# Both rope products of a key in one GpSimd instruction, behind two ScalarE copies

## The chip, the cores and the metric

The kernel runs on one core of a Trainium2 chip. A core has a matrix engine (TensorE, PE in the profile; its weight loads are PEld), a vector engine (VectorE, DVE), an activation engine (ScalarE, ACT), a general engine (GpSimd, POOL) and an engine that only issues transfers (SyncE, SP). Each works through its own queue in order; they meet at semaphores. The metric is the device time of one execution in microseconds, as the median of several runs.

## What is computed

One transformer block over 2048 tokens of width 256, in float32: attention with a compressed key-value path and rotary positions, a residual and a layer norm; then a mixture of 16 experts, of which each token takes two, with a shared expert, a residual and a second layer norm. Cut to what the change touches:

```python
q = (x @ Wq) ...                      # 16 heads of 16, 4 without rotation, 12 with
c_kv = x @ Wkv_down                   # 64 wide
k = (c_kv @ Wk_up) ...
v = (c_kv @ Wv_up) ...
q_rope, k_rope = _apply_rope(q_rope, cos, sin), _apply_rope(k_rope, cos, sin)
scores = jnp.einsum('bhqd,bhkd->bhqk', qf, kf) * scale    # causal
out = jnp.einsum('bhqk,bhkd->bhqd', softmax(scores), v)
```

A rotated key is the sum of two products: the plain projection times a table of cosines, and a projection with its even and odd columns exchanged times a table of signed sines.

## The kernel before

Tokens are taken in four chunks of 512 (`CH`), heads in four groups of four (`G`). The channels of a head are padded to 32 rows (`PAD`), so a group of four heads fills 128 partitions. Everything about keys and queries lies with channels on partitions and tokens along the free dimension, as 128x512 tiles.

For each group `g` and chunk `c`, `project_k` (L422) makes a key tile. PE writes two PSUM banks `pk[0]` and `pk[1]` (the plain and the exchanged projection; 64 rows of weights each). DVE reads `pk[0]`, adds the column `unit` (a one in one row of each head, which carries the softmax shift later) and multiplies by the cosines `cs[c][:, 0]` (L430). For the very first key DVE also does the second product (L434). For the other 15, ACT copies `pk[1]` to SBUF (L436), since POOL doesn't read PSUM, and POOL multiplies that copy by the sines in place (L437). Then POOL adds the halves into the key (L439). The two halves are the two planes of one tile `tmp`, named `rot` in the profile, of which there is one buffer.

Queries are made likewise (`project_q`: copy on ACT, L452, product on POOL, L453), values by `project_v` (ACT, L468).

The attention itself is a list of steps, written out by hand (`steps`, L605 to L669). A step may hold a `Maxima` part and a `Weighted` part. `Maxima` computes scores of four heads with the queries as rows (`m`), only to find the row maxima: DVE reduces each bank (L505), or, on the diagonal, masks and reduces it (L500). `Weighted` computes scores with the keys as rows (`s`); ACT takes the exponential (L550), and on the diagonal POOL masks it (L554). The product with the values (`av`) of a step is put on PE after the scores of the step that follows; ACT copies it out (`more`, L581, two buffers) and POOL adds it to a sum (L582), or DVE adds it from PSUM where a step has no maxima (L578).

The maxima are turned by PE and added to the queries (`shift`, L515 to L523, `qa`). Projections are hung behind steps by number (`put`, L683 to L719): the keys of group `g` come 14, 11, 8 and 6 steps ahead of the first maxima step of that group's last chunk.

All PSUM of this stage is one pool of eight banks taken in turn (`bank`, L404; tag `sc`). So a matmul that takes a bank waits until what took that bank eight takings earlier has been read. In a full step the takings are `s` and `m` of heads in turns (two `s`, two `m`, two `s`, two `m`), then `av`, then whatever is hung behind the step. Matmuls keep their written order (L142); the other engines' queues are ordered when the program is built, by what is ready. Each float32 product is two passes on PE.

At the start, weights and rope tables come over SP's queue (L350 to L382), and POOL copies parts of the weights of groups 1 to 3 as they land (`double`, L339, hung behind step 5).

Of the kernel before, what the change touches and what calls it, by code (L numbers as in the profile page):

```python
# [12 lines left out]
AF = mybir.ActivationFunctionType  # L13
ALU = mybir.AluOpType
# [36 lines left out]
def block_kernel(  # L51
# [14 lines left out]
    nc = tc.nc  # L66
# [25 lines left out]
    cs = [const.tile([P, 2, CH], F32, tag=f"cs{c}", name=f"cs{c}") for c in range(3)]  # L92
# [52 lines left out]
    def matmul(*args, **kw):  # L145
        pe(nc.tensor.matmul, *args, **kw)
# [142 lines left out]
    with ExitStack() as att:  # L289
# [14 lines left out]
        unit = ap1.tile([P, 1], F32, tag="unit", name="unit")  # L304
# [99 lines left out]
        def bank(name):  # L404
            return ps_sc.tile([P, CH], F32, tag="sc", name=name)
# [16 lines left out]
        def project_k(g, c):  # L422
            tmp = wk1.tile([P, 2, CH], F32, tag="rot", name=f"rot{g}_{c}")
            pk = [bank(f"pk{g}_{c}_{a}") for a in range(2)]
            for a in range(2):
                r = slice(a * LAT, (a + 1) * LAT)
                matmul(
                    pk[a], lhsT=wks[g][r], rhs=ckv[c][r], start=True, stop=True
                )
            nc.vector.scalar_tensor_tensor(  # L430
                tmp[:, 0, :], pk[0], unit, cs[c][:, 0, :], ALU.add, ALU.mult
            )
            if (g, c) == (0, 0):
                nc.vector.tensor_tensor(tmp[:, 1, :], pk[1], cs[c][:, 1, :], ALU.mult)  # L434
            else:
                nc.scalar.copy(tmp[:, 1, :], pk[1])  # L436
                nc.gpsimd.tensor_tensor(tmp[:, 1, :], tmp[:, 1, :], cs[c][:, 1, :], ALU.mult)  # L437
            ks[g, c] = kv.tile([P, CH], F32, tag="k", name=f"k{g}_{c}")
            nc.gpsimd.tensor_tensor(ks[g, c], tmp[:, 0, :], tmp[:, 1, :], ALU.add)  # L439

# [245 lines left out]
        for step, what, c in (  # L686
            (1, project_k, 1), (1, project_q, 1), (3, prologue, 2), (4, project_v, 0),
            (6, project_k, 2), (7, prologue, 3), (9, project_v, 1), (9, project_q, 2),
            (14, project_k, 3), (17, project_q, 3), (19, project_v, 2), (32, project_v, 3),
        ):  # L690
            if what is prologue:
                put(step, what, c)
            else:
                put(step, what, 0, c)
# [498 lines left out]
```

## Time and profile before

| what | value |
|---|---|
| three runs | 780.91, 782.22, 784.98 us; median 782.22 |
| the profiled execution | 787.57 us, span 785.7 us |
| mean granted TensorE clock | 0.979 |
| ACT, exponentials (L550), 640 | 292.2 us busy |
| DVE, maxima off the diagonal (L505), 384 | 238.2 us busy, 0.683 each |
| POOL, sums of value products (L582), 125 | 136.8 us busy; 1.270 at 512 columns, 0.727 at 256 |
| DVE, first product of a key (L430), 16 | 12.0 us busy |
| ACT, copy of the second half (L436), 15 | 8.8 us busy |
| POOL, second product (L437), 15 | 19.1 us busy |
| POOL, sum of the halves (L439), 16 | 20.3 us busy |

A line of the timeline gives the start, the duration, the engine, the line of the kernel, the operation with its output and input, how many of it are merged, and in brackets how long the engine had been idle and which instruction ended that. A line of the table by stage gives the stretch, its length, then the busy time and number of instructions of PE, PEld, DVE, ACT and POOL, the granted clock, the DMA share and the GB/s. In a tile's view the three durations are the least, the median and the largest in ns, and "who waited for it" gives microseconds and times. Matmuls overlap and their ends are modelled, so PE's busy share overstates how hard it works.

### The profile page before, as it was taken

What the parts mean: (1) busy time and instruction counts of PE and PEld (TensorE: products, weight loads), DVE (VectorE), ACT (ScalarE), POOL (GpSimd) and SP (SyncE); (2) the same over time, 40 slices, a digit from 0 to 9 for tenths busy, and PEclk for the clock granted to TensorE, in tenths of its full rate; (3) what the DMA queues carried; (4) which work ended last, traced back from release to release, by engine and by line L of the source; (5) the groups of instructions that cost most, each with busy time, mean ns of one, the idle gap of its engine ahead of it and who ended that gap; (6) DMA issues with size and microseconds to landing.
All of it is one profiled execution on the core that took longest, in us unless ns stands there. A gap on an engine that the chain in (4) does not pass through costs nothing.

```text
span 785.7 us, 14672 instructions
## 1 busy us (share of the span) xinstructions
PE 754.0 (96%) x5074; PEld 366.7 (47%) x5074; DVE 525.0 (67%) x1435; ACT 453.6 (58%) x987; POOL 359.9 (46%) x589
## 2 busy tenths in 40 slices
PE   7999999999999999999999999999998989999994
PEld 3444443444434334443434454444333658887542
DVE  2658798887687787767787768788657633333275
ACT  1244747377786787777788767875553202223356
POOL 3234536535377454657645564553446124445300
PEclk9999999989999999999999999998989999999998
DMA  5469999998000000001000000000115543332172
GB/s 148 131 149 263 300 291 291 293 308 214 2 1 1 1 1 3 1 4 36 20 1 1 2 1 2 2 1 2 55 55 144 112 123 102 112 105 64 29 225 98
DMA packets 75981, 72.54 MB, mean 92 GB/s; under 512 B 20890, under 2 KB 70141, under 8 KB 75904
## 3 DMA queue, kind: packets, MB, share of 16 engines
q1 hardware_dynamic: 70936, 62.43, 29.9%
q0 software_dynamic: 3504, 8.43, 3.2%
q10 hardware_dynamic: 1464, 0.72, 0.4%
q8 instruction: 41, 0.67, 0.4%
q14 instruction: 36, 0.29, 0.1%
HBM read 27.09 MB, written 45.65 MB: 93 GB/s over the span
## 4 chain that ended last, share of the span: by engine, by line
PE 81%; SPq 5%; DVE 4%; DMA 3%; issue 3%; ACT 2%; POOL 1%; ACTq 0%; POOLq 0%; DVEq 0%
PE s L143 23%; PE av L143 18%; PE m L143 16%; PE py L143 4%; PE ab L143 4%; PE pq L143 3%; PE c L143 2%; PE pk L143 2%; PE ph L143 2%; SPq L326 1%; PE pv L143 1%; SPq L325 1%; PE pz L143 1%; PE px L143 1%; PE h L143 1%
## 5 line engine op out<-in xcount | busy, mean ns | idle before, releaser
L550 ACT ACTIVATE p<-s 128x512 f32<-128x512 f32 (+3 forms) x640 | 292.2, 540 | 93.9 <-PE m L143 48.8
L143 PE MATMUL m<-k,q 32*128 32x512 f32 (+3 forms) x1280 | 298.0, 570 | 0.7 <-DVE rot L430 0.5
L143 PE MATMUL s<-qa,k 32*128 32x512 f32 (+3 forms) x1280 | 282.9, 569 | 3.5 <-DVE avs L578 2.5
L505 DVE TENSOR_REDUCE pm<-m 128x1 f32<-128x512 f32 x384 | 238.2, 683 | 61.1 <-PE m L143 59.9
L582 POOL TENSOR_TENSOR avs<-avs,more 128x512 f32<-128x512 f32 (+3 forms) x125 | 136.8, 1094 | 140.2 <-ACT more L581 136.5
L143 PEld LDWEIGHTS s<-qa,k 32*128 32x128 f32 x1280 | 108.8, 187 | 120.9 <-ACT p L550 69.1
L143 PE MATMUL av<-p,v 128*32 128x512 f32 (+3 forms) x1280 | 158.7, 551 | 1.6 <-POOL p L554 0.6
L500 DVE CUSTOM_DVE_ANT_0 m<-m,qmask 128x512 f32<-128x512 f32 (+3 forms) x256 | 118.5, 522 | 37.2 <-PE m L143 34.0
L143 PEld LDWEIGHTS m<-k,q 32*128 32x128 f32 x1280 | 120.2, 184 | 38.3 <-issue 12.0
L554 POOL TENSOR_SCALAR_AFFINE_SELECT p<-p 128x128 f32<-128x128 f32 x256 | 70.3, 296 | 36.8 <-ACT p L550 35.1
L581 ACT COPY more<-av 128x512 f32<-128x512 f32 (+3 forms) x125 | 65.8, 526 | 34.8 <-PE av L143 27.9
L143 PEld LDWEIGHTS av<-p,v 128*32 128x32 f32 x1280 | 27.9, 108 | 107.3 <-ACT p L550 53.6
L954 POOL DMA_INDIRECT yg<-yb,to x41 | 40.4, 986 | 71.5 <-ACT yb L942 50.6
L281 POOL DMA_INDIRECT xg<-xr,slot x32 | 31.1, 973 | 33.2 <-issue 21.2
L143 PE MATMUL h<-xT,cs 128*128 128x512 f32 (+1 forms) x96 | 43.3, 597 | 2.4 <-ACT u L808 1.4
L143 PE MATMUL py<-w2r,hT 112*128 112x256 f32 (+1 forms) x164 | 39.8, 380 | 0.0
L500 DVE DVE_READ_ACCUMULATOR2_ANT pm<- 128x1 f32 x256 | 36.2, 142 | 0.0
L143 PEld LDWEIGHTS py<-w2r,hT 112*128 112x128 f32 x164 | 30.8, 190 | 6.1 <-ACT hT L993 0.5
L143 PE MATMUL ab<-xT,w 128*112 128x256 f32 x128 | 32.9, 380 | 0.0
L143 PE MATMUL pq<-xT,wqs 128*128 128x512 f32 x64 | 31.7, 618 | 0.0
L143 PEld LDWEIGHTS h<-xT,cs 128*128 128x128 f32 (+1 forms) x96 | 16.9, 180 | 24.2 <-issue 18.8
L437 POOL TENSOR_TENSOR rot<-rot,cs 128x512 f32<-128x512 f32 x15 | 19.1, 1273 | 17.1 <-DMA cq<-in_rope_dram 7.4
(166 smaller groups left out, 651.8 us busy)
## 6 DMA issues: line engine op xcount, KB each, us to landing
xg<-hot SPq DMA_DIRECT2D x16, 2064.0 KB
xb<-xg SPq DMA_DIRECT2D x16, 258.0 KB
got<-yg SPq DMA_DIRECT2D x8, 512.0 KB
w<-in_w_dram SPq DMA_DIRECT2D x4, 896.0 KB
xr<-in_x_dram SPq DMA_DIRECT2D x4, 512.0 KB
w<-in_w_dram SPq DMA_DIRECT2D x4, 512.0 KB
out_dram<-o SPq DMA_DIRECT2D x8, 256.0 KB
w2r<-in_w_dram SPq DMA_DIRECT2D x1, 1792.0 KB
```

The costliest lines, as they stand in the source:

```text
L143: tc.keep_in_program_order(op(*args, **kw))
L281: put = nc.gpsimd.indirect_dma_start(out=xg[:, :], out_offset=bass.IndirectOffsetOnAxis(ap=slot[:, j, i : i + 1], axis=0), in_=xr[c][:, t, ...
L325: queue.dma_start(out=cs[c][r : r + LOW], in_=of[:LOW])
L326: queue.dma_start(out=cs[c][r + LOW : r + PAD], in_=of[NOPE:HD])
L437: nc.gpsimd.tensor_tensor(tmp[:, 1, :], tmp[:, 1, :], cs[c][:, 1, :], ALU.mult)
L500: nc.vector.tensor_tensor_reduce(out=ps[:, :n], in0=ps[:, :n], in1=qmask[:, CH - n :], scale=1.0, scalar=3.0 * NEG, op0=ALU.add, op1=ALU.m ...
L505: nc.vector.tensor_reduce(to, ps, AX.X, ALU.max)
L550: nc.scalar.activation(pr[:, n0:], ps[:, n0:], AF.Exp, scale=SCALE)
L554: nc.gpsimd.affine_select(out=diag, in_=diag, pattern=[[1, P]], base=0, channel_multiplier=-1, compare_op=ALU.is_ge, fill=0.0,)
L581: nc.scalar.copy(more[:, n0:], pv[:, n0:])
L582: nc.gpsimd.tensor_tensor(to, to, more[:, n0:], ALU.add)
L954: nc.gpsimd.indirect_dma_start(out=yg[:, :], out_offset=bass.IndirectOffsetOnAxis(ap=to, axis=0), in_=yb, in_offset=None, bounds_check=2 * ...
```

## The change

For 15 of the 16 keys the addition of `unit` and the first product leave DVE. ACT now makes two copies, the first an Identity with `unit` as its bias, and POOL multiplies both planes of `tmp` by both planes of the rope table in one instruction of 1024 columns. The first key stays as it was. The sum of the halves isn't touched.

```diff
-            nc.vector.scalar_tensor_tensor(
-                tmp[:, 0, :], pk[0], unit, cs[c][:, 0, :], ALU.add, ALU.mult
-            )
             if (g, c) == (0, 0):
+                nc.vector.scalar_tensor_tensor(
+                    tmp[:, 0, :], pk[0], unit, cs[c][:, 0, :], ALU.add, ALU.mult
+                )
                 nc.vector.tensor_tensor(tmp[:, 1, :], pk[1], cs[c][:, 1, :], ALU.mult)
             else:
+                nc.scalar.activation(tmp[:, 0, :], pk[0], AF.Identity, bias=unit)
                 nc.scalar.copy(tmp[:, 1, :], pk[1])
-                nc.gpsimd.tensor_tensor(tmp[:, 1, :], tmp[:, 1, :], cs[c][:, 1, :], ALU.mult)
+                nc.gpsimd.tensor_tensor(tmp, tmp, cs[c], ALU.mult)
             ks[g, c] = kv.tile([P, CH], F32, tag="k", name=f"k{g}_{c}")
             nc.gpsimd.tensor_tensor(ks[g, c], tmp[:, 0, :], tmp[:, 1, :], ALU.add)
```

## The prediction

> **What bounds the kernel now.** I read the page's busy shares, then its chain of waits, then the busy time by stage, then the tile view of the two projections of a key, and last the timeline around each of the 15 changed keys.
>
> ```profile
> PE 754.0 (96%) x5074; PEld 366.7 (47%) x5074; DVE 525.0 (67%) x1435; ACT 453.6 (58%) x987; POOL 359.9 (46%) x589
> PE 81%; SPq 5%; DVE 4%; DMA 3%; issue 3%; ACT 2%; POOL 1%; ACTq 0%; POOLq 0%; DVEq 0%
> 216.00:250.00 34.00, 33.75 (x280) 13.20 (x276) 26.39 (x64) 26.51 (x59) 24.82 (x33) 1.00 0.00 1
> ```
>
> PE holds 81% of the chain, DVE 4%. In the stretch 216 to 250 us, which contains four changed keys, PE is busy 33.75 of 34 us, DVE 26.4, ACT 26.5, POOL 24.8. So the work taken from DVE is mostly work nobody waits for; what counts is what PE waits for. The tile view of `pk` says that:
>
> ```profile
> L430 DVE SCALAR_TENSOR_TENSOR rot<-pk,unit,cs x16: 741/751/752, 14.2 to 378.2; 128x512 f32<-128x512 f32 x16
> L436 ACT COPY rot<-pk x15: 586/586/587, 23.7 to 378.2; 128x512 f32<-128x512 f32 x15
> ...
>   PEld m L143: 3.9, 14
> ```
>
> The last line stands under "who waited for it": PE waits 3.9 us in 14 places for `pk` to be read. The reason is the ring of eight PSUM banks: the two banks of `pk` are the last two taken in their step, so eight takings later they come up as the last two `m` products of the next step. What PE waits for is the reading of `pk`, not the key: in every pass but the first the finished key is wanted several steps later.
>
> **The terms taken away and added, per key.** DVE loses one 0.75 us instruction (15 x 0.75 = 11.2 us). ACT gains one Identity. The trace has no Identity of 128x512 with one column operand. From below, the copy of this shape takes 0.586 and the exponential 0.602. From above, the Identity of 128x256 with two column operands (L1042) takes 0.591 against 0.384 for the Silu of 112x256 without any (L927): 0.207 for two, so 0.10 for one, and 0.81 if one cost as much as both. I take 0.60 + 0.10 = 0.70, bounds 0.59 to 0.81. POOL's multiplication goes from 512 to 1024 columns: by L582 at 256 and 512 columns (0.727 and 1.270) a column costs 2.12 ns, so 1.27 + 512 x 2.12 = 2.36 us, 1.09 more; from above two instructions, 2.54; from below 2.3, as the three widths of L582 lie on one line. ACT's four exponentials of 0.602 take 2.07 together, so each starts 0.11 before its forerunner ends.
>
> **Before 52 us: nothing.** Two changed keys lie here (reads at 23.7 and 39.5 us). The stretch ends with POOL copying weights that arrive late behind the issues of the SP queue, and with PE's `av` behind that:
>
> ```profile
> 51.25 0.39 POOL L348 COPY wqs<-sines 128x48 f32<-128x48 f32 x2 [1.60 <-DMA sines<-in_wq_dram]
> 51.59 0.55 POOL L554 TENSOR_SCALAR_AFFINE_SELECT p<-p 128x128 f32<-128x128 f32 x2
> 51.94 1.98 PE L143 MATMUL av<-p,v 128*32 128x512 f32 x5 [0.44 <-POOL p L554]
> ```
>
> The chain runs through SP's issues from 17.4 to 48.3 us, and the change issues no DMA and adds none behind which one waits. POOL idles 3.3 us before 47.2, so the 1.7 us by which a key gets later (Identity's 0.70 less the overlap of 0.11, and POOL's 1.09) is covered; without that cover it would cost up to 1.7 each.
>
> **Two keys where DVE is the limit: a gain.** At 70.5 and 105.8 us the steps are without exponentials before, and DVE works without a gap:
>
> ```profile
> 68.13 2.48 DVE L505 TENSOR_REDUCE pm<-m 128x1 f32<-128x512 f32 x4
> 70.53 0.74 DVE L430 SCALAR_TENSOR_TENSOR rot<-pk,unit,cs 128x512 f32<-128x512 f32 x1
> 71.18 2.58 DVE L505 TENSOR_REDUCE pm<-m 128x1 f32<-128x512 f32 x4
> ```
>
> The last four `m` start at 71.32, right behind L430. ACT is free from 68.23 and would have read both banks by 69.4, so those matmuls can follow the last `s` (70.66 plus the 0.1 to 0.2 that separates starts). That is 0.5 us each; bounds 0 (the exponentials on ACT start 69.42 anyway) and 0.65, DVE's start to start. Two: -1.0.
>
> **Nine keys in full steps: a loss.** From 116 to 371 us the read of `pk` stands in a gap of both engines. Around 230 us:
>
> ```profile
> 230.10 0.59 ACT L436 COPY rot<-pk 128x512 f32<-128x512 f32 x1 [0.42 <-PE pk L143]
> 230.13 0.75 DVE L430 SCALAR_TENSOR_TENSOR rot<-pk,unit,cs 128x512 f32<-128x512 f32 x1 [0.66 <-PE pk L143]
> 230.93 0.18 PEld L143 LDWEIGHTS m<-k,q 32*128 32x128 f32 x1 [0.23 <-DVE rot L430]
> 231.11 2.07 ACT L550 ACTIVATE p<-s 128x512 f32<-128x512 f32 x4 [0.43 <-PE m L143]
> 231.99 0.16 PEld L143 LDWEIGHTS av<-p,v 128*32 128x32 f32 x8 [0.76 <-issue]
> ```
>
> Now the banks are read side by side, free at 230.69 and 230.88. After the change ACT reads them in turn: Identity 230.10 to 230.80, copy from 230.69 to 231.28. The first `m` loses nothing, the second starts at 231.33, not 230.94. Behind it in PE's queue is `av`, which needs all rows and so waits for it. The second pass of that `m` moves from 231.46 to at least 231.33 + 0.43 = 231.76. PE is late by 0.30 to 0.39; I take 0.35. ACT's exponentials start at 231.17, not 231.11: nothing. DVE gains nothing, as its next reduction waits 0.32 for PE already. Lateness of a PE that is busy all the time isn't made up. Bounds per key: 0.2 (Identity at 0.59, passes closing up) and 0.5 (Identity at 0.81). Nine: +3.15.
>
> **Two keys ahead of a diagonal step of 128 columns: a loss on POOL.** At 246 and 378 us POOL's queue holds the mask of the next values product:
>
> ```profile
> 247.34 1.28 POOL L437 TENSOR_TENSOR rot<-rot,cs 128x512 f32<-128x512 f32 x1
> 248.56 0.30 POOL L554 TENSOR_SCALAR_AFFINE_SELECT p<-p 128x128 f32<-128x128 f32 x1
> 248.83 1.27 POOL L439 TENSOR_TENSOR k<-rot 128x512 f32<-128x512 f32 x1
> 250.04 0.80 POOL L554 TENSOR_SCALAR_AFFINE_SELECT p<-p 128x128 f32<-128x128 f32 x3
> ```
>
> PE's `av` on these masks runs from 250.65 to 251.24, so there is no slack. After: copies end 247.55, product 247.60 to 249.96, one mask to 250.23, the add to 251.5, the other masks to 252.3, `av` done near 252.6. That is 1.35 late (the PE lateness of the paragraph above lies inside it). If the order of POOL's queue changes so that all four masks precede the add, they end at 251.05 and 0.35 remains; upper bound 1.75, with the product at 2.54 and Identity at 0.81. Two: +2.7. Elsewhere the masks have room: at 137 us they would end near 139.5, with their `av` at 140.15.
>
> **Sum.** -1.0 + 3.15 + 2.7 = +4.85 us. The profiled execution took 787.57 us (span 785.7), which is 5.35 above the median of 782.22; I add the sum to the median: 787.1. By the bounds: +0.7 x 2 - 1.3 + 1.8 - 0.7 = +1.2 to 0 + 4.5 + 3.5 = +8.0, so 783.4 to 790.2.
>
> **A rule weighed.** Identity between exponentials could bring table loads. In the trace the Identity at 761.98 follows a Silu and that at 774.67 a Sqrt, neither with a load, so I count none. A load, where there is one, takes 1.28 us, and the Silu at 761.49 starts 0.02 after it. The Trainium skill, "ScalarE: Activation LUTs", What ACT_TABLE_LOAD costs, adds a drain of 1.38 us to each switch, 2.66 in all; the trace shows no such drain. A pair of loads at each of 13 keys would cost 13 x 2 x 1.28 = 33 us by the row. By that page it would be 69.
>
> **The rivals.**
> 1. Faster, 0.17. PE's waits on L430 vanish and nothing takes their place, because ACT has the second copy done before PE comes to that `m`. For it: ACT idles 0.4 on both sides of the copy in most places. Against: the two reads together last 1.18 us, and PE arrives 0.84 after the first begins. It decides at 0.84 for both reads. Price: the 3.9 us of `pk` waits and 1.0 of the DVE stretch go: 777.3.
> 2. Lost in the noise, 0.13. PE's lateness is taken up by the small gaps ahead of later `av`, and POOL puts the masks first: -1.0 + 9 x 0.1 + 2 x 0.35 = +0.6: 782.8.
> 3. POOL becomes the bound, 0.08. Its queue delays every `avs` sum, the two `more` buffers fill, ACT waits. POOL's load in 216 to 250 rises by 4 x 1.09 to 29.2 of 34 us, which speaks against it. 13 keys x 1.7 = +22: 804.3.
> 4. Identity brings a pair of table loads at each key, 0.02: 13 x 2 x 1.28 = +33: 815.6.
>
> **The numbers.** The forecast has 0.60; a time is told from no change at 0.5%, 3.9 us. The slower threshold, 786.1, cuts the forecast's own range (783.4 to 790.2) so that three quarters of it lie above: 0.45 slower, 0.15 same. With rivals 3 and 4 slower is 0.55, with rival 2 same is 0.28, faster is 0.17. The range runs from 779, which leaves out rival 1's own time but not half of its gain, to 792, which leaves out rivals 3 and 4.
>
> **What would show it.** After the change: no DVE row for L430 but one; an Identity row near 0.70 and a POOL product near 2.36; PE's second `m` behind ACT's copy in nine places, waiting some 0.4; `av` behind POOL's masks at 246 and 378; the DVE gaps at 70 and 106 gone. If the waits for the copy stay below 0.1, or the masks come ahead of the add, I am wrong towards rivals 1 and 2; a long wait of ACT's `more` on POOL would be rival 3.

## The result, and the profile after

| | before | after |
|---|---|---|
| median of 20 runs | 781.49 us (777.09 to 784.98) | 786.80 us (781.28 to 789.55) |
| ratio after to before | | 1.0055, interval 1.0038 to 1.0071 |
| the profiled execution, its span | 787.57, 785.7 us | 787.13, 785.2 us |
| granted clock of that execution | 0.979 | 0.984 |

By the ratio the change makes the kernel slower by 4.3 us, 3.0 to 5.5 by the interval. (The two medians differ by 5.3 us and the means of the same runs by 4.2.) The two profiled executions don't show it in their spans, because the clock differed between them; the last section comes to that. So the spans are not compared here, but places in them.

The first two lines are from the page after: the busy shares and the chain of waits. The third is the table by stage for the stretch shown before (stretch, length, busy time and instructions of PE, PEld, DVE, ACT and POOL, clock, DMA share, GB/s).

```profile
PE 755.3 (96%) x5074; PEld 368.3 (47%) x5074; DVE 513.9 (65%) x1420; ACT 461.9 (59%) x1002; POOL 375.9 (48%) x589
PE 84%; DVE 6%; DMA 3%; ACT 2%; issue 2%; POOL 2%; SPq 0%; ACTq 0%; POOLq 0%; DVEq 0%
216.00:250.00 34.00, 33.83 (x272) 13.47 (x271) 23.36 (x59) 27.91 (x62) 27.41 (x31) 1.00 0.01 1
```

DVE has lost 11.1 us of work, ACT has gained 8.3 and POOL 16.0. POOL's 27.41 us in the stretch hold two instructions fewer than before, which have moved out at its end. PE's share of the chain is still above 80%. Nothing in these three lines says why the kernel got slower.

The tile view of the projections of a key has the new durations (least, median, largest in ns, first and last start), and the group of POOL's product its mean:

```profile
L436 ACT ACTIVATE rot<-pk,unit x15: 687/688/688, 22.7 to 380.6; 128x512 f32<-128x512 f32 x15
L437 ACT COPY rot<-pk x15: 577/577/582, 23.2 to 381.2; 128x512 f32<-128x512 f32 x15
...
  PEld m L143: 2.1, 10
```

```profile
L438 POOL TENSOR_TENSOR rot<-rot,cs 128x1024 f32<-128x1024 f32 x15 | 35.4, 2361 | 21.8 <-ACT rot L437 11.5
```

The last line of the tile view is a trap. PE's waits for `pk` went from 3.9 us to 2.1, and yet PE comes later at this very place. The timeline around 230 us, where before was shown too (start, duration, engine, line, operation, idle time in brackets), says how:

```profile
230.19 0.69 ACT L436 ACTIVATE rot<-pk,unit 128x512 f32<-128x512 f32 x1 [0.38 <-PE pk L143]
230.78 0.58 ACT L437 COPY rot<-pk 128x512 f32<-128x512 f32 x1
230.93 0.31 PEld L143 LDWEIGHTS m<-k,q 32*128 32x128 f32 x2
231.25 2.07 ACT L551 ACTIVATE p<-s 128x512 f32<-128x512 f32 x4
231.40 0.29 PEld L143 LDWEIGHTS m<-k,q 32*128 32x128 f32 x2
231.94 0.59 PE L143 MATMUL m<-k,q 32*128 32x512 f32 x1
232.45 0.16 PEld L143 LDWEIGHTS av<-p,v 128*32 128x32 f32 x8 [0.76 <-issue]
```

The second bank is read from 230.78 to 231.36. The last two `m` start at 231.40, 0.47 after the pair before them (230.93), as the loads show. Before, all four had been let go by 231.04. The matmuls that wait sit between others that run, so hardly any of the delay is booked as idle time; it shows in the starts. This step's scores began at 229.95 before and its `av` at 231.99, 2.04 us later. Now it is 230.09 and 232.45: 2.36.

For the whole stage I took the starts of the same matmuls in both traces (the first of each `pk`, and of the transposes `pn`, `pq` and `po`) and subtracted: PE's lateness against the trace of before, at places that hold the same work. What counts is by how much it changes from one place to the next: a cell says by how much PE's lateness grew (+) or shrank (-) around that time. Below, "e1" to "e8" are the experiments of the next section; all numbers are us.

| around | after | e1 | e2 | e3 | e4 | e8 |
|---|---|---|---|---|---|---|
| 70 and 106, each | -0.62 | 0.00 | -0.61 | -0.61 | -0.61 | -0.17 |
| 116, 125, 132, 219, 349, each | +0.38 to +0.42 | -0.12 to +0.04 | +0.38 to +0.42 | +0.38 to +0.42 | -0.02 to 0 | -0.03 to 0, once -0.10 |
| 230, 360, each | +0.28 | 0 | +0.28 | +0.28 | 0 | 0 |
| 239, 371, each | +0.02 | 0 | +0.02 | +0.02 | 0 | 0 |
| 246 | +1.33 | +1.02 | +0.26 | -0.03 | -0.06 | +1.04 |
| 378 | +1.08 | +0.99 | +0.39 | -0.10 | 0.00 | +0.76 |

The column "after" adds up to -1.24 + 2.57 + 2.41 = +3.7 us, against 4.3 (3.0 to 5.5) in the times.

Left out of this sum is the stretch from 155 to 186 us, in which no key is made. There PE comes 0.59 us earlier after the change than before. Between 150 and 160 us the granted clock was 0.73 in the trace of before and 1.00 in the trace after. In each of the eight other traces that have 1.00 there PE gains the same 0.59, whatever the kernel, and in e10, the kernel before once more with 0.71, it gains nothing. In e2 and e4, with 0.72 and 0.80 there, it comes 0.1 and 1.9 later. So this is put down to the clock and not to the change.

At 246 the loss is POOL's:

```profile
248.03 2.36 POOL L438 TENSOR_TENSOR rot<-rot,cs 128x1024 f32<-128x1024 f32 x1 [0.27 <-ACT rot L437]
250.34 0.29 POOL L555 TENSOR_SCALAR_AFFINE_SELECT p<-p 128x128 f32<-128x128 f32 x1
250.60 1.26 POOL L440 TENSOR_TENSOR k<-rot 128x512 f32<-128x512 f32 x1
251.82 0.79 POOL L555 TENSOR_SCALAR_AFFINE_SELECT p<-p 128x128 f32<-128x128 f32 x3
252.17 0.91 PE L143 MATMUL av<-p,v 128*32 128x128 f32 x6 [0.42 <-POOL p L555]
```

One product of 2.36 us stands ahead of four masks that ACT's exponentials had made ready by 248.63, and the sum of the halves stands between the masks, which end at 252.61. PE's `av` follows the last mask it wants, with 0.42 us of idle time that is put down to POOL. At 68 to 73 us the gain is DVE's:

```profile
68.47 0.69 ACT L436 ACTIVATE rot<-pk,unit 128x512 f32<-128x512 f32 x1 [4.59 <-PE pk L143]
68.51 5.02 DVE L506 TENSOR_REDUCE pm<-m 128x1 f32<-128x512 f32 x8
71.04 0.70 PE L143 MATMUL m<-k,q 32*128 32x512 f32 x2
72.10 0.65 PE L143 MATMUL po<-ident,avs 128*128 128x128 f32 x4
```

The 4 + 4 reductions with the product between them (68.13 to 73.76 before) have become one row of eight in 5.02 us.

### The profile page after: what moved, and what is told of

Its sections match the earlier page's. It is cut to its first block, busy times and chain, and to the rows that moved or that the text cites. A ratio compares the mean times of both kernels' runs of the same rounds, so it can differ in the third digit from the quotient of the medians.

```text
span 785.2 us, 14644 instructions
## 1 busy us (share of the span) xinstructions
PE 755.3 (96%) x5074; PEld 368.3 (47%) x5074; DVE 513.9 (65%) x1420; ACT 461.9 (59%) x1002; POOL 375.9 (48%) x589
## 4 chain that ended last, share of the span: by engine, by line
PE 84%; DVE 6%; DMA 3%; ACT 2%; issue 2%; POOL 2%; SPq 0%; ACTq 0%; POOLq 0%; DVEq 0%
PE s L143 21%; PE av L143 17%; PE m L143 17%; PE py L143 4%; PE pq L143 4%; PE ab L143 4%; PE h L143 2%; PE c L143 2%; PE pk L143 2%; PE ph L143 2%; PE pv L143 1%; PE px L143 1%; PE pz L143 1%; DVE pm L506 1%; PE pc L143 1%
## 5 line engine op out<-in xcount | busy, mean ns | idle before, releaser
L143 PE MATMUL s<-qa,k 32*128 32x512 f32 (+3 forms) x1280 | 279.0, 558 | 1.8 <-DVE avs L579 0.7
L143 PEld LDWEIGHTS s<-qa,k 32*128 32x128 f32 x1280 | 106.8, 185 | 117.6 <-ACT p L551 69.5
L143 PE MATMUL av<-p,v 128*32 128x512 f32 (+3 forms) x1280 | 156.8, 546 | 2.7 <-DVE base L247 1.2
L143 PEld LDWEIGHTS m<-k,q 32*128 32x128 f32 x1280 | 122.0, 183 | 40.6 <-issue 12.5
L438 POOL TENSOR_TENSOR rot<-rot,cs 128x1024 f32<-128x1024 f32 x15 | 35.4, 2361 | 21.8 <-ACT rot L437 11.5
```

The lines of the kernel that those rows point to most:

```text
L143: tc.keep_in_program_order(op(*args, **kw))
L438: nc.gpsimd.tensor_tensor(tmp, tmp, cs[c], ALU.mult)
```

## The experiments

My theory after the result: the loss is that ACT reads the two banks in turn (nine keys), and that POOL's longer product holds up the masks (two keys); the gain is DVE's at two keys. The rivals: it is POOL's product alone, or ACT's added work alone. Kernels of one group below ran on one chip beside the kernel before. Its median was 787.00 us beside e1 to e4, 783.21 beside e5 to e8, and 787.78 beside e9 to e11.

**e1: the unit row added by DVE.** ACT's Identity goes; POOL's product of 1024 columns stays. The banks are read by two engines again.

```diff
-                nc.scalar.activation(tmp[:, 0, :], pk[0], AF.Identity, bias=unit)
+                nc.vector.tensor_scalar(tmp[:, 0, :], pk[0], unit, None, ALU.add)
                 nc.scalar.copy(tmp[:, 1, :], pk[1])
                 nc.gpsimd.tensor_tensor(tmp, tmp, cs[c], ALU.mult)
```

> DVE again reads the first bank, but only adds unit; ACT copies the second; POOL multiplies both planes in one instruction of 1024 columns. So the banks are read side by side as before and POOL's queue is that of after. My theory (late reads of pk, and masks behind a longer POOL product): the masks' share alone is left, +1.33 and +1.10 at 246 and 378 us, +2.4 in all against before, ratio 1.003; PE's second m behind pk is not late anywhere, and no gain at 70 and 106. Rival, all of the loss is POOL's 16 us: about +5, ratio 1.006. Rival, ACT's extra 9 us: 0, ratio 1.000.

Measured: 788.25 us, ratio 1.0026, interval 1.0011 to 1.0040. The timeline at 228 us:

```profile
228.68 0.59 ACT L437 COPY rot<-pk 128x512 f32<-128x512 f32 x1 [0.42 <-PE pk L143]
228.71 0.75 DVE L436 TENSOR_SCALAR rot<-pk,unit 128x512 f32<-128x512 f32 x1 [0.66 <-PE pk L143]
...
230.57 0.16 PEld L143 LDWEIGHTS av<-p,v 128*32 128x32 f32 x8 [0.76 <-issue]
```

Both banks are read side by side, and `av` follows the first score (228.53) by 2.04 us, as in the kernel before. The nine steps cost nothing and the two gains at 70 and 106 are gone; the two waits for masks are there, 1.02 and 0.99. Both rivals fall: POOL's longer product alone isn't the whole loss (1.006 was expected for that), and it isn't nothing (1.000).

**e2: POOL's short product.** The cosine product of 15 keys is left out, so that only POOL's time differs from the changed kernel.

```diff
-                nc.gpsimd.tensor_tensor(tmp, tmp, cs[c], ALU.mult)
+                nc.gpsimd.tensor_tensor(tmp[:, 1, :], tmp[:, 1, :], cs[c][:, 1, :], ALU.mult)
```

> As after, but POOL multiplies the second plane alone: the product with the cosines is left out for 15 keys, and so POOL's times are those of before. Theory: the reads of pk alone, -1.2 at 70 and 106 and +2.6 at the nine full steps, +1.4 in all, ratio 1.002; some 0.3 each at 246 and 378 in place of 1.1 to 1.3. POOL rival: only the gain, -1.2, ratio 0.998. ACT rival: the whole loss, +4 to +5, ratio 1.006.

Measured: 787.42 us, 1.0015, interval 0.9999 to 1.0031. POOL's queue at 248:

```profile
248.00 1.28 POOL L438 TENSOR_TENSOR rot<-rot,cs 128x512 f32<-128x512 f32 x1 [0.28 <-ACT rot L437]
...
250.71 0.80 POOL L555 TENSOR_SCALAR_AFFINE_SELECT p<-p 128x128 f32<-128x128 f32 x3
```

The last masks start 1.1 us earlier than after the change. At 246 and 378 only what the reads cost is left (0.26 and 0.39); it too comes by way of POOL, whose product starts when the second copy has ended. Every other place repeats the changed kernel. The traces add up to -1.22 + 2.57 + 0.65 = +2.0, within the interval of the times. The interval includes no change, but not the ratios of the two rivals (0.998 and 1.006).

**e3 and e6: the key one step later.** In groups 2 and 3 the last key is hung one step further on, so that it no longer stands ahead of the narrow diagonal step. The two are one kernel, on two chips.

```diff
-                put(i + (-14, -11, -8, -6)[c], project_k, g, c)
+                put(i + (-14, -11, -8, -5 if g > 1 else -6)[c], project_k, g, c)
```

> As after, with the key of the last chunk of groups 2 and 3 projected one step later, behind the diagonal step of 128 columns and not ahead of it; its masks then stand ahead of the product in POOL's queue. Theory: PE's wait for the masks at 252 and 384 us is gone, 2.4 less than after: +1.4 to +2 against before, ratio 1.002. Both rivals: as after, +4 to +5, ratio 1.0055.

> The changed kernel with the last key of groups 2 and 3 one step later, once more. From its first trace +1.3 against before up to 525 us, ratio 1.0017, though it measured 1.0034: 2.4 us less than the changed kernel beside it if the masks are the cause, the same as it if not.

Measured: e3 789.39 us, 1.0034, interval 1.0021 to 1.0048; e6 783.04 us, 1.0004, interval 0.9984 to 1.0024. POOL's queue of e3 at the same step:

```profile
246.92 1.04 POOL L555 TENSOR_SCALAR_AFFINE_SELECT p<-p 128x128 f32<-128x128 f32 x4
247.97 1.26 POOL L583 TENSOR_TENSOR avs<-avs,more 128x512 f32<-128x512 f32 x1
249.44 2.36 POOL L438 TENSOR_TENSOR rot<-rot,cs 128x1024 f32<-128x1024 f32 x1 [0.21 <-ACT rot L437]
251.88 1.26 POOL L440 TENSOR_TENSOR k<-rot 128x512 f32<-128x512 f32 x1
```

All four masks precede the product, and the steps of 1.33 and 1.08 are gone from PE's lateness. From 67 to 525 us it adds up to +1.2, which is 2.5 below the changed kernel (1.33 + 0.03 and 1.08 + 0.10) and would be a ratio of 1.0015. The interval of e6 holds that, the one of e3 lies just above it; the two intervals overlap by a hair, and the mean of the two ratios is 1.0019. The changed kernel itself ran beside e6 on the same chip (e5, below): it took 786.19 us, 3.2 more than e6, where 2.4 were expected.

**e7: the same move in the kernel before.** It asks whether the move gains by itself.

> The kernel before with the same move of two keys, as the control: the masks of 246 and 378 us were on the edge there, not late, so 0.0 to -0.2, ratio 1.000. If the move itself gains 2 us, e6 says nothing on the masks.

Measured: 781.31 us, 0.9977, interval 0.9961 to 0.9993. In PE's lateness -0.41 at 246, -0.16 at 378, nothing elsewhere. The masks had been waited for a little already, and the move takes that too. So 0.57 of what e3 wins isn't the change's loss. I had expected 0.0 to -0.2.

**e4 and e11: the new form for the four early keys alone.** The keys at 70 and 106 us are among them, and two ahead of 52 us.

```diff
-            if (g, c) == (0, 0):
...
+            if (g, c) in ((0, 1), (0, 2), (0, 3), (1, 0)):
                 nc.scalar.activation(tmp[:, 0, :], pk[0], AF.Identity, bias=unit)
                 nc.scalar.copy(tmp[:, 1, :], pk[1])
                 nc.gpsimd.tensor_tensor(tmp, tmp, cs[c], ALU.mult)
+            else:
+                nc.vector.scalar_tensor_tensor(
+                    tmp[:, 0, :], pk[0], unit, cs[c][:, 0, :], ALU.add, ALU.mult
+                )
...
```

> The new form only for the four keys that are made while DVE is the limit or the start waits for transfers ((0,1), (0,2), (0,3), (1,0)); the other eleven as before. Theory: -0.6 at each of 70 and 106 us, nothing before 52, so -1.2, ratio 0.9985. POOL and ACT rivals: 4 of 15 of the loss, +1.3, ratio 1.0017.

> The new form for the four early keys alone, once more: -1.2, ratio 0.9985.

Measured: e4 785.46 us, 0.9986, interval 0.9970 to 1.0003; e11 (the same kernel, another chip) 785.09 us, 0.9967, interval 0.9951 to 0.9982. In the trace of e4 PE's lateness changes by -0.61 at each of the two keys, by -0.06 at 246 and by no more than 0.02 at the other ten places. The sign is settled by e11; the size stands between the trace's 1.3 us and the 2.6 of e11.

**e5: the changed kernel again.**

> The changed kernel itself, on the same chip as the three below. From PE's lateness in its trace (-1.2 at 70 and 106, +2.6 at nine full steps, +2.4 at 246 and 378): +3.8 against before, ratio 1.0048. If the time beyond 525 us belongs to the change too, more.

Measured: 786.19 us, 1.0034, interval 1.0017 to 1.0052. Its lateness repeats the column "after" within 0.02 us (-0.61 and -0.62 at the two early keys, +1.35 and +1.07 at the two late ones).

**e8: the second bank copied by DVE.** Identity stays on ACT, POOL's product too. If it is Identity that costs PE time, the nine steps stay late; if it is reading in turn, they don't.

```diff
                 nc.scalar.activation(tmp[:, 0, :], pk[0], AF.Identity, bias=unit)
-                nc.scalar.copy(tmp[:, 1, :], pk[1])
+                nc.vector.tensor_copy(tmp[:, 1, :], pk[1])
```

> As after, but the second bank is copied by DVE, beside ACT's Identity on the first: POOL's product is still 1024 columns. Theory (it is the reading in turn that makes PE late, not the Identity): 0 at the nine full steps; DVE is back in the path at 70 and 106, so no gain there; masks still late at 246 and 378, up to 1.0 each (POOL's queue has two masks ahead of the product here). +1 to +2, ratio 1.002. If Identity itself is what is late: +2.6 more, ratio 1.005.

Measured: 781.98 us, 0.9986, interval 0.9972 to 1.0001. The timeline at 227 us:

```profile
227.50 0.69 ACT L436 ACTIVATE rot<-pk,unit 128x512 f32<-128x512 f32 x1 [0.38 <-PE pk L143]
227.61 0.69 DVE L437 COPY rot<-pk 128x512 f32<-128x512 f32 x1 [0.70 <-PE pk L143]
...
229.40 0.16 PEld L143 LDWEIGHTS av<-p,v 128*32 128x32 f32 x8 [0.76 <-issue]
```

With the banks read side by side, `av` comes 2.00 us after the first score (227.40), although Identity is there. The nine steps cost nothing. So what costs PE time is that one engine reads both banks in turn, not Identity. The lateness adds up to about +1.3 us, but the medians differ by -1.2. The clock accounts for most of this gap: the mean granted clock was 0.988 in the twelve executions of e8 and 0.985 in the 35 of the kernel before beside them. A straight line of time against clock through all 47, with an offset for e8, gives an offset of +0.7 us (about 0.1 to 1.4).

**e9: early keys alone, and the late key moved.** The edits of e4 and e3 together.

> The two parts that gained, together: the new form for the four early keys only, and the last key of groups 2 and 3 one step later. In the traces -1.2 and -0.6: -1.8 against before, ratio 0.9977. If the gain of the move (0.9977 by its times, more than its trace shows) is real in full, -3.0, ratio 0.996.

Measured: 785.00 us, 0.9965, interval 0.9948 to 0.9983. The lateness adds up to -0.60 - 0.62 - 0.39 - 0.16 = -1.8 us. It is faster than the kernel before, as e11 is; the times don't separate the two (785.00 and 785.09).

**e10: the kernel before against itself.**

> The kernel before, as if it were a changed one: ratio 1.000. How far it falls from 1.000 is what a ratio of this size is worth: the theory takes the traces' lateness as the truth, and expects up to 0.0015 either way; the rival, that the times know something the traces don't, expects less than 0.0005.

Measured: 788.05 us, 1.0008, interval 0.9992 to 1.0024. From 66 to 525 us no matmul of the trace moves by more than 0.02 us against the first trace of before. Behind that, where the clock dips, it moves by more (0.08 at 597 us). Ahead of it there is a shift of -0.53 at 65 us, with nothing changed.

## Why the prediction was right

The time of 787.1 us was forecast and 786.8 measured; the ratio forecast was 1.006 (4.85 of 782.2), the measured one is 1.0055. By its steps:

- **The new terms.** Identity was taken at 0.70 and takes 0.688; POOL's product was taken at 2.36 and takes 2.361. The Trainium skill, "ScalarE: Activation LUTs", What ACT_TABLE_LOAD costs, gives some 93 ns for a column operand of an ACTIVATE; here Identity takes 85 ns more than an exponential of the same shape without one (688 less 603), which is close to that, and 111 more than the copy behind it (688 less 577). No table load was added: both traces have eleven.
- **Before 52 us: nothing.** The lateness at 65 us is +0.4 in the trace after and +0.9 in e5, the same kernel. It is -0.5 in e10, which changes nothing, -1.3 in e4 and -0.7 in e11, which are one kernel, and -1.5 in e8. So a cost or gain of up to some 1 us can't be told here, and none shows.
- **Two DVE-limited keys, -0.5 each.** Measured -0.62 each, in four traces alike; e1 takes it away by leaving work of 0.75 us on DVE.
- **Nine full steps, +0.35 each.** Five cost 0.38 to 0.42, two 0.28, and two nothing: 2.57 for all, against 3.15. Reading in turn is the cause (e1 and e8, from both sides). The sentence that failed is "Lateness of a PE that is busy all the time isn't made up". At 239 and 371 it is made up within the next step. The timelines at 240, before and then after:

```profile
240.54 5.08 DVE L505 TENSOR_REDUCE pm<-m 128x1 f32<-128x512 f32 x8 [0.32 <-PE m L143]
...
241.90 0.70 PE L143 MATMUL s<-qa,k 32*128 32x512 f32 x2
...
243.08 0.30 PEld L143 LDWEIGHTS m<-k,q 32*128 32x128 f32 x4
...
244.14 1.06 PE L143 MATMUL av<-p,v 128*32 128x512 f32 x8
```

```profile
240.95 2.48 DVE L506 TENSOR_REDUCE pm<-m 128x1 f32<-128x512 f32 x4 [2.23 <-PE m L143]
...
242.64 0.70 PE L143 MATMUL s<-qa,k 32*128 32x512 f32 x2
...
243.49 0.31 PEld L143 LDWEIGHTS m<-k,q 32*128 32x128 f32 x4
...
244.57 1.06 PE L143 MATMUL av<-p,v 128*32 128x512 f32 x8
```

  The third `m` of the second step takes the bank of the last `m` of the first step, so its load waits until DVE's fourth reduction has read that bank. That reduction ended at 243.03 before and ends at 243.43 after (240.95 + 2.48), and the load follows at 243.08 and 243.49. DVE's reductions are only 0.41 us later than before, and by that much PE was late already ahead of this key (at 238). PE comes to the second step 0.74 us late (241.90 and 242.64), but it would have waited there for DVE anyway: the step takes 1.93 us, where it took 2.24, and at its `av` PE is 0.43 late. That is what rival 2 spoke of, lateness taken up in a later step. How much is taken up goes with the columns of the `av` between the two steps: nothing at 512 (five keys), a part at 384 (230 and 360), all at 256 (239 and 371). The forecast's "DVE gains nothing" holds; what it left out is that PE has a wait for DVE in the step behind.
- **Two keys ahead of the narrow diagonal step, +1.35 each.** Measured +1.33 and +1.08. Of these 0.26 and 0.39 are the reads (e2) and the rest is POOL's longer product, as predicted; with the masks first the loss is gone (e3). At 378 PE is at first 1.40 late, and 0.32 of it is taken up within 4 us.
- **The signs to look for.** PE's wait for the copy was expected at 0.4 in nine places. As a booked wait it is not there: PE's booked waits on `pk` fell. It is there in the starts. A reader who had gone by the waits alone would have decided for rival 1.
- **The other rivals.** POOL didn't become the bound: it is 48% busy, and in the tile view of `more` no instruction of ACT waits for POOL's sums. Table loads didn't come.

So the mechanisms were right, but for the lateness that is made up, and the sum was 1.1 us too large by the traces (4.85 against 3.7). The nearness of 787.1 to 786.8 is partly luck: 786.8 is the median of runs between 781.3 and 789.6, and the sum was added to a median of three runs, 782.22, that lies 0.73 above the median of twenty.

Open: the traces of e3, e8 and e11 add up to sums outside the intervals of their times (1.0015, 1.0017 and 0.9984 as ratios), e3's too low, the other two too high; those of the other runs lie inside or at the edge. One kernel on two chips differs by 1.5 us (e4 and e11) and 2.4 us (e3 and e6). The clocks of the single executions explain a part of this. The table sets beside the traces' sums the differences in time at equal clock: a straight line of time against mean clock through the executions of a run and of the kernel before beside it, with an offset for the run, as for e8 above (± is about 95%; all in us).

| | e1 | e2 | e3 | e6 | e4 | e11 | e5 | e7 | e8 | e9 | e10 |
|---|---|---|---|---|---|---|---|---|---|---|---|
| traces | +1.9 | +2.0 | +1.2 | +1.2 | -1.3 | -1.3 | +3.7 | -0.6 | +1.3 | -1.8 | 0 |
| times at equal clock | +1.7 | +1.4 | +2.1 | +0.5 | -1.0 | -1.9 | +3.7 | -1.1 | +0.7 | -2.0 | +0.2 |
| ± | 0.8 | 0.7 | 0.7 | 0.6 | 0.6 | 0.8 | 0.7 | 0.5 | 0.6 | 0.8 | 0.7 |

So e8 and e11 come to agree with their traces; e3 and e6, which are one kernel, lie a little above and a little below theirs, and e7 at the edge. Whether a kernel by itself moves the clock isn't shown, and for the kernel before in the twenty runs of the result the clocks are not on record.

## What to carry to other kernels

Where two engines used to read two PSUM banks side by side and one engine now reads them in turn, the second bank comes free later, and the matmul that takes it next in the ring starts later. The price (0.28 to 0.42 us at seven of nine keys here) is hardly booked as a wait, and has to be read from the starts of the same matmuls in both traces. It vanishes where TensorE would have waited soon after for something that hasn't become later. Work taken from an engine that isn't the bound can still pay at the few places where it is, so give the new form to those alone: given to four of fifteen keys it gained (clear of the noise in e11, not in e4), given to all fifteen it lost. Before work on a side engine is made longer, look at what stands behind it in its queue at the narrowest step.

## What the runs showed of the hardware

The granted clock hides differences of this size. The table by stage of before, and then of after:

```profile
150.00:160.00 10.00, 10.00 (x40) 6.32 (x42) 9.97 (x18) 1.32 (x3) 1.20 (x2) 0.73 1.09 303
530.00:550.00 20.00, 20.00 (x153) 9.41 (x156) 16.08 (x78) 11.06 (x28) 6.81 (x23) 0.83 0.01 2
570.00:580.00 10.00, 9.51 (x46) 2.63 (x46) 5.94 (x20) 5.31 (x11) 4.82 (x5) 0.66 0.16 54
```

```profile
150.00:160.00 10.00, 10.00 (x43) 5.24 (x44) 9.97 (x19) 2.28 (x4) 1.20 (x2) 1.00 1.10 330
530.00:550.00 20.00, 19.35 (x169) 9.50 (x163) 17.07 (x87) 12.36 (x35) 8.89 (x27) 1.00 0.01 2
570.00:580.00 10.00, 8.81 (x55) 2.54 (x54) 6.26 (x22) 5.14 (x11) 4.80 (x5) 0.83 0.19 66
```

The clock column (the third from the end) falls to 0.66 to 0.83 for stretches of 10 to 20 us, in some executions and not in others. At 525 us PE is 3.5 us later after the change than before. At 598 us it is 2.6 us earlier, and the two dips between were deeper before: by an estimate from the clock column (1.00 - 0.83) x 20 + (0.83 - 0.66) x 10 = 5.1 of these 6.1 us. So the two spans agree while the medians don't. From 150 to 160 us the same reckoning would give 2.7 us, but there the dip cost PE only 0.59: DVE was busy for 9.97 of the 10 us, which fits that DVE and not PE's clock set the pace. In the 20 runs of the changed kernel the time follows the mean clock: 0.994 went with 781.3 us, 0.984 with 787.1, 0.979 with 788.3; a straight line through all 20 falls by 5.1 us for each 0.01, with a correlation of -0.97. For the kernel before, beside the experiments, the fall was smaller: 2.3 us on two chips and 3.6 on the third, with correlations of -0.7 to -0.84.

From 66 to 525 us the starts of all matmuls of a trace repeat to 0.02 us when the same kernel runs again, but for one shift common to all (e5 against the trace after, e10 against the trace before). An effect of 0.3 us that no time could tell from noise is plain in it.
